# Where a VectorE block transposition stands in a group's order: slots 4 and 6, or slots 6 and 7

## The chip, the core and the metric

The kernel runs on one core of a Trainium2 chip. The metric is the device time of one execution in microseconds; lower is better. Before the change it is 1522.22 us, the median of three runs from 1521.25 to 1522.27.

The core has engines that work side by side, each with a queue of its own in program order: TensorE (PE, matrix products; PEld in the profile is its weight load), VectorE (DVE), ScalarE (ACT), GpSimd (POOL), and the queue of SyncE (SP), from which transfers are issued. They synchronise through semaphores. Products land in PSUM, which has eight banks.

## The reference

A batch is a matrix x of 128 nodes by 512 features; there are 128 batches. Two layers follow each other, both over the same adjacency matrix `adj` (128 x 128):

```python
h = jnp.maximum(_layernorm(x, axis=-1), 0.0)
x = x + _L0_gnn_ref(h, adj, adj, b0)      # W1 = W2 = adj
h = jnp.maximum(_layernorm(x, axis=-1), 0.0)
x = x + _L1_gnn_ref(h, adj, Wq, bq, Wk, bk, Wv, bv)
```

The first layer comes down to one number per node, `max(max_j (adj @ h)[i, j] + b0[i], 0)`, since A and C - A cancel but for the bias. Added to a whole row of x, it does not change that row's layer norm, so the second layer can use the same h. The second layer is attention with 8 heads of 64 over the 128 nodes, with scores masked where `adj` is zero: q, k and v are h times 512 x 512 weights.

## The kernel before

**Tiling.** Four batches are a group; there are 32 groups. The loop over g (lines 701 to 762) does, for each group: `apply` (weights times v of the group before, L600), `scores` (k times q, L570), and then the products that make v of group g and q and k of group g+1.

**Products.** A 512 x 512 projection of a group is cut into 2 x 2 quarters and done with seven quarter products instead of eight (class `Products`, lines 392 to 536; matmuls at L421, 128 x 256 each). Two of the seven, p4 and p3, are cut again into small blocks of 128 x 128 (`p43a` and `p43b`, matmuls at L487). The results are collected in PSUM banks and in the sum tile `u` by VectorE additions: L460 after p6, L469 after p7, L442 after p5 and at the end, and L490 (`more`), which adds a small block from the scratch bank 6 (`scr`) to `u`. Since `scr` is used several times, a small product into it must wait until the L490 addition of the one before has read it.

**Slots.** The work of a group is an explicit list `part` of 18 slots: v in slots 0 to 5, q in 6 to 11, k in 12 to 17. In each six stand p1, p6, p2, p7 with p43a, p5, p43b. In the first and the last group v has plain p7, p5, p4 and p3 instead of the block form. After the products of slot s, everything in `todo[s]` is issued. This is the order by hand in which each engine's queue gets its instructions: a matmul waits only for its data, but behind a VectorE instruction in the queue stands whatever was issued later.

**Side work in the slots.** While group g is computed, group g+2 is prepared. m = 4g + 8 is its first batch. `next_norms(m)` says in which slot each step of that stands, and is used as long as there is a group g+2, so in the first 30 groups:

- `norm` (L279 to L286): statistics on VectorE, then two small steps on GpSimd. `norm_end` (L289): the normalised rows with a relu on ScalarE, into tile `hn`.
- `add_bv` (L295, GpSimd): adds v's bias to x in place, for the sum at the end.
- `blocks` (L302, VectorE): transposes `hn` of one batch in blocks of 32 x 32 into tile `tb`.
- `move` (L312, SP): 16 transfers that bring the blocks of a pair of batches to their places in tile `hT`, so that `hT` holds the transposed matrix. It follows the second batch of a pair.
- `adjacency` (L327 on TensorE into bank 7, then the reduction L328 on VectorE).

In the same slots stand the masks of the attention weights (L582, on GpSimd, in the last groups on VectorE), the quarter sums of the next group (L345 on VectorE, L359 on GpSimd), loads of x (L229) and `add_c` (L626, ScalarE).

Of the kernel before, what the change touches and what calls it, by code (L numbers as in the profile page):

```python
# [167 lines left out]
def tile_adj_preln_d2(  # L168
# [38 lines left out]
    def fast(ctx):  # L207
# [436 lines left out]
        def next_norms(m):  # L644

            return {
                0: [(norm_end, m, False), (norm_end, m + 1, False)],
                4: [(blocks, m)],
                6: [(blocks, m + 1), (move, m + 1), (add_bv, m), (add_bv, m + 1)], 7: [(adjacency, m)],
                8: [(norm, m + 2), (norm_end, m + 2)],  # L650
                12: [(norm, m + 3), (norm_end, m + 3), (adjacency, m + 1)],
                13: [(blocks, m + 2)],
                14: [(blocks, m + 3), (move, m + 3), (adjacency, m + 2)],
            }

        with tc.manual_schedule():
# [44 lines left out]
            for g in range(NG):  # L701
# [16 lines left out]
                m = b + 2 * G  # L718
                if g + 1 < NG:
# [12 lines left out]
                    if g + 2 < NG:  # L732
                        for s, l in next_norms(m).items():
                            for what in l:
                                add(s, *what)
                    else:
                        add(6, count, 0, b)
# [73 lines left out]
```

## Time and profile before

| what | value |
|---|---|
| time, median of three runs | 1522.22 us |
| span of the profiled execution | 1519.2 us |
| one group in the middle (750.66 to 797.41) | 46.75 us |
| of it busy: TensorE, VectorE, ScalarE, GpSimd | 46.75, 31.62, 15.73, 26.66 us |
| transposition L302: count, median | 124, 701 ns |
| issues of `move` L312: count, median | 992, 609 ns |
| idle time of VectorE before L490, ended by L487 | 111.3 us in all |

"Busy" is the time in which an engine has an instruction running. The chain of waits follows the execution back from its end, at each step to what released it; its pieces in order of time show how long TensorE spent on each stretch of equal matmuls. The timeline lists single instructions: start in us from the span's start, length in us, engine, line, operation, output and inputs, and in brackets the idle time ahead of it and what ended it. A 32-bit matmul appears as two records, so that a quarter product of four matmuls reads "x8".

### The profile page before, as it was taken

How to read it: one execution, taken by the hardware profiler on the slowest of the kernel's cores; microseconds unless marked ns; L12 is line 12 of the kernel's file. 1: busy time of each engine (PE TensorE's matmuls, PEld its weight loads, DVE VectorE, ACT ScalarE, POOL GpSimd, SP SyncE). 2: the span in 40 equal slices, each digit the busy share in tenths (PEclk: the TensorE clock that was granted, in tenths of full speed). 3: DMA queues.
4: the chain of work that ended last, by engine and by line, in shares of the span. 5: the costliest groups of instructions: out<-in, count | busy, mean ns of one | idle time of the engine just before them, and what ended most of it. 6: DMA issues, size and time to landing. Idle time of an engine off the chain costs nothing.

```text
span 1519.2 us, 33036 instructions
## 1 busy us (share of the span) xinstructions
PE 1504.1 (99%) x12909; PEld 1325.6 (87%) x12909; DVE 1023.2 (67%) x2187; ACT 507.3 (33%) x970; POOL 844.4 (56%) x968
## 2 busy tenths in 40 slices
PE   8999999999999999999999999999999999999997
PEld 6888888888889888888888888888988888888886
DVE  6666666666666767666666666666676766666666
ACT  4333323333243332333332333324333233333232
POOL 5675656556565555654565655656555565456520
PEclk9999999999999999999999999999999999999999
DMA  5223222223222232222322222322223222222201
GB/s 170 58 65 80 59 65 74 65 76 75 52 73 67 73 83 43 76 66 74 80 58 65 75 65 76 73 54 73 66 73 84 43 76 76 64 80 57 52 32 58
DMA packets 307807, 105.32 MB, mean 69 GB/s; under 512 B 273153, under 2 KB 273281, under 8 KB 307649
## 3 DMA queue, kind: packets, MB, share of 16 engines
q1 hardware_dynamic: 307328, 102.84, 26.3%
q8 instruction: 104, 1.70, 0.5%
q14 instruction: 55, 0.44, 0.1%
q0 software_dynamic: 176, 0.27, 0.1%
q10 hardware_dynamic: 144, 0.07, 0.0%
HBM read 37.03 MB, written 33.55 MB: 46 GB/s over the span
## 4 chain that ended last, share of the span: by engine, by line
PE 99%; DVE 0%; DMA 0%; POOL 0%; ACT 0%; DVEq 0%; issue 0%
PE bk L421 55%; PE bk L487 19%; PE bk L600 8%; PE bk L570 8%; PE bk L327 7%; PE bk L546 1%; PE bk L321 0%; DMA xp<-in_x_dram 0%; DVE o L618 0%; ACT o L289 0%; DVE live L639 0%; DVE st L279 0%; DVE RS L617 0%; DVE o L630 0%; DVEq L776 0%; POOL rstd L284 0%
## 5 line engine op out<-in xcount | busy, mean ns | idle before, releaser
L630 POOL TENSOR_TENSOR o<-xp,o 128x512 f32<-128x512 f32 x122 | 151.1, 1268 | 312.7 <-DVE o L618 269.4
L582 POOL TENSOR_TENSOR w<-w,live 128x512 f32<-128x512 f32 x240 | 297.6, 1272 | 0.0
L490 DVE TENSOR_TENSOR u<-u,bk 128x256 f32<-128x256 f32 x552 | 205.7, 414 | 115.4 <-PE bk L487 111.3
L578 ACT ACTIVATE w<-bk 128x512 f32<-128x512 f32 x256 | 128.8, 625 | 345.6 <-PE bk L570 345.6
L295 POOL TENSOR_TENSOR xp<-xp,bv_sb 128x512 f32<-128x512 f32 x128 | 161.1, 1269 | 59.5 <-ACT hn L289 58.6
L421 PEld LDWEIGHTS bk<-hs,sk_sb 128*128 128x128 f32 x768 | 143.6, 190 | 44.7 <-issue 29.4
L421 PE MATMUL bk<-hs,sk_sb 128*128 128x256 f32 x768 | 181.3, 379 | 0.0
L421 PE MATMUL bk<-sv_sb,hs 128*128 128x256 f32 x768 | 181.2, 379 | 0.0
L421 PE MATMUL bk<-hs,sq_sb 128*128 128x256 f32 x744 | 175.8, 379 | 0.0
L421 PEld LDWEIGHTS bk<-sv_sb,hs 128*128 128x128 f32 x768 | 143.6, 190 | 31.1 <-issue 14.3
L328 DVE TENSOR_REDUCE amax<-bk 128x1 f32<-128x512 f32 x128 | 88.2, 689 | 105.4 <-PE bk L327 102.5
L359 POOL TENSOR_TENSOR h<-hT 128x256 f32<-128x256 f32 x31 | 22.6, 728 | 238.2 <-PE bk L487 233.8
L421 PEld LDWEIGHTS bk<-hs,sq_sb 128*128 128x128 f32 x744 | 138.9, 190 | 17.7
L469 DVE TENSOR_TENSOR u<-bk,u 128x512 f32<-128x512 f32 x95 | 65.8, 692 | 116.7 <-PE bk L421 114.6
L289 ACT ACTIVATE hn<-xp,nmr,rstd 128x512 f32<-128x512 f32 x124 | 100.8, 813 | 104.8 <-POOL nmr L286 104.8
L327 PE MATMUL bk<-hn,adjT 128*128 128x512 f32 x248 | 126.6, 592 | 0.0
L600 PE MATMUL bk<-v,w 128*64 128x65 f32 x4096 | 126.5, 222 | 0.0
L600 PEld LDWEIGHTS bk<-v,w 128*64 128x64 f32 x4096 | 122.1, 137 | 4.1 <-issue 0.3
L421 PE MATMUL bk<-wv_sb,hT 128*128 128x256 f32 x512 | 124.3, 386 | 0.0
L570 PE MATMUL bk<-qT,kT 64*128 64x128 f32 x2048 | 122.9, 275 | 0.0
L421 PE MATMUL bk<-hT,wk_sb 128*128 128x256 f32 x512 | 121.2, 380 | 0.0
L570 PEld LDWEIGHTS bk<-qT,kT 64*128 64x128 f32 x2048 | 116.8, 188 | 2.5 <-issue 0.3
(149 smaller groups left out, 2575.1 us busy)
## 6 DMA issues: line engine op xcount, KB each, us to landing
out_dram<-o SPq DMA_DIRECT2D x128, 256.0 KB, 2.0
xp<-in_x_dram SPq DMA_DIRECT2D x62, 512.0 KB, 3.9
hT<-tb SPq DMA_DIRECT2D x992, 32.0 KB, 1.9
xp<-in_x_dram SPq DMA_DIRECT2D x4, 256.0 KB, 4.4
wq_sb<-in_L_gnn_Wq_dram SPq DMA_DIRECT2D x2, 512.0 KB, 8.2
wk_sb<-in_L_gnn_Wk_dram SPq DMA_DIRECT2D x2, 512.0 KB, 9.8
wv_sb<-in_L_gnn_Wv_dram SPq DMA_DIRECT2D x2, 512.0 KB, 10.5
bv_sb<-in_L_gnn_bv_dram POOLq DMA_DIRECT2D x1, 256.0 KB, 6.7
```

The lines of the kernel that those rows point to most:

```text
L289: nc.scalar.activation(HN[m], x_of(m), AF.Relu, scale=RSTD[m], bias=NMR[m])
L295: nc.gpsimd.tensor_tensor(x_m, x_m, bv_sb, op=ALU.add)
L327: nc.tensor.matmul(pa, adjT, HN[m], start=True, stop=True)
L328: nc.vector.reduce_max(AMAX[g][:, i : i + 1], pa, axis=AX.X)
L421: nc.tensor.matmul(bank[:, r, :], lhs, rhs, start=first and r == 0 and c == 0, stop=r == 1 and c == 1, skip_group_check=True,)
L487: nc.tensor.matmul(out, lhs, rhs, start=start, stop=True, skip_group_check=True)
L490: nc.vector.tensor_tensor(to, to, what, op=ALU.add)
L570: nc.tensor.matmul(psc[j][:, f, :], KT[g][r, f, i * D : (i + 1) * D], QT[g][r, f, i * D : (i + 1) * D], start=True, stop=True,)
L578: nc.scalar.activation(w[:, j], psc[j], AF.Exp, scale=HD ** -0.5)
L582: eng.tensor_tensor(w[:, j], w[:, j], live_h, op=ALU.mult)
L600: nc.tensor.matmul(pav[r, c : c + HE], w[:, h % 2, h // 2, r], V[:, i, h, :], start=True, stop=True,)
L630: eng.tensor_tensor(y, x_of(b), y, op=ALU.add)
```

## The change

The transposition of batch m leaves slot 4 for slot 6, that of batch m+1 leaves slot 6 for slot 7. The `move` of the pair, which needs both, goes with the second. The two `add_bv` stay in slot 6. In VectorE's order this brings batch m's transposition from ahead of v's last L490 and L442 additions to behind them, and batch m+1's from ahead of q's p6 addition to behind it, ahead of the reduction of `adjacency(m)`. It is meant to keep VectorE free for the additions at the end of v, for which TensorE's products may have to wait. The transpositions of the other two batches (slots 13 and 14) stay.

```diff
             return {
                 0: [(norm_end, m, False), (norm_end, m + 1, False)],
-                4: [(blocks, m)],
-                6: [(blocks, m + 1), (move, m + 1), (add_bv, m), (add_bv, m + 1)], 7: [(adjacency, m)],
+                6: [(blocks, m), (add_bv, m), (add_bv, m + 1)],
+                7: [(blocks, m + 1), (move, m + 1), (adjacency, m)],
                 8: [(norm, m + 2), (norm_end, m + 2)],
                 12: [(norm, m + 3), (norm_end, m + 3), (adjacency, m + 1)],
                 13: [(blocks, m + 2)],
```

## The prediction

> **What bounds the kernel now.** I read the page's busy times and its chain first, then the chain in order of time over one group, then the timelines of TensorE and VectorE in that group.
>
> ```profile
> PE 1504.1 (99%) x12909; PEld 1325.6 (87%) x12909; DVE 1023.2 (67%) x2187; ACT 507.3 (33%) x970; POOL 844.4 (56%) x968
> PE 99%; DVE 0%; DMA 0%; POOL 0%; ACT 0%; DVEq 0%; issue 0%
> ```
>
> TensorE (PE) is busy 99% of the span and is 99% of the chain. The table of stretches says it more sharply: a group in the middle lasts 46.75 us, and PE is busy 46.75 us of it. VectorE (DVE) has 31.6 us, GpSimd (POOL) 26.7 and ScalarE (ACT) 15.7 of those 46.75. So nothing counts unless it shortens TensorE's own sequence. The list of waits names no steady wait of PE. But a matmul that is held up can hide in that busy time: the end of a record is modelled, and a piece of the chain runs to the next start. So I compared equal pieces. Here is one group in the chain in order of time (start, length, piece):
>
> ```profile
> 756.74 1.73 PE bk L421 x8
> 758.46 2.42 PE bk L487 x20
> 760.88 3.46 PE bk L421 x16
> ...
> 771.27 2.23 PE bk L487 x20
> ...
> 784.75 2.23 PE bk L487 x20
> ```
>
> The three pieces L487 x20 are the same work (`p43b`, ten 128x128 products, each recorded twice) for v, q and k. For v it takes 2.42 us, for q and k 2.23: 0.19 us too long. It repeats in every group from the second to the second-last; one q piece of the 30th group has 2.33. The timelines of DVE, PE and the weight loads (PEld), first at v's slots 4 and 5, then at q's slots 10 and 11:
>
> ```profile
> 758.50 0.69 DVE L442 TENSOR_TENSOR v<-bk,u 128x512 f32<-128x512 f32 x1 [0.65 <-PE bk L421]
> 759.11 0.70 DVE L302 STREAM_TRANSPOSE tb<-hn 128x512 f32<-128x512 f32 x1
> 759.74 0.38 DVE L490 TENSOR_TENSOR u<-u,bk 128x256 f32<-128x256 f32 x1
> 760.17 0.52 PEld L487 LDWEIGHTS bk<-ssv_sb,h 128*128 128x128 f32 x4
> 760.17 0.71 PE L487 MATMUL bk<-ssv_sb,h 128*128 128x128 f32 x4
> ...
> 771.31 0.69 DVE L442 TENSOR_TENSOR qT<-bk,u 128x512 f32<-128x512 f32 x1 [0.65 <-PE bk L421]
> 771.91 0.41 DVE L490 TENSOR_TENSOR u<-u,bk 128x256 f32<-128x256 f32 x1
> 772.78 0.53 PEld L487 LDWEIGHTS bk<-h,ssq_sb 128*128 128x128 f32 x4
> 772.89 0.61 PE L487 MATMUL bk<-h,ssq_sb 128*128 128x128 f32 x4
> ```
>
> In q the L490 addition follows p5's addition at once. It ends at 772.32, and the last products into bank 6 start undisturbed, the weight load 0.11 us before the matmul. In v the transposition of block m stands between. The addition, which reads bank 6, ends at 760.12. Only then, 0.05 us later, does the load of the next products into bank 6 start, together with its matmul. Undisturbed, the load would follow the one before (759.75) by 0.22 us, the spacing in this piece, at 759.97. So 0.20 us by these rounded times, 0.19 by the pieces: TensorE waits for VectorE here.
>
> **What the Trainium skill says.** "Perfetto Trace Analysis", section "Tensor Engine Instruction (MATMUL, LD_WEIGHTS)": the profiler estimates a matmul's end, and DVE, ACT and GpSimd queues are strict FIFO. The trace agrees: busy time equals the period although 0.19 us is lost, and the L490 addition doesn't start before the transposition ahead of it. "TensorE: Matmul & The Clock Gate", "Step-by-step: what each phase is for": PE may pull weight loads ahead of running matmuls, but matmuls keep program order. Here loads lead by 0.11 us, and at 760.17 the lead is zero. "SBUF — State Buffer", "Who interferes with whom": a DVE instruction with at most one SBUF input, outside the two-port modes, doesn't contend with GpSimd. The trace fits: GpSimd's 128x256 subtraction takes 0.73 us at 760.97 without a transposition beside it, and 0.73 us at 762.73 with one.
>
> **The change, part by part.**
>
> *Removed from slot 4.* In v's slots 4 and 5 DVE no longer has the transposition, 0.63 us from its start to that of the next instruction (759.11 to 759.74). The L490 addition starts at 759.11 and ends at about 759.5, against 759.92 that the weight load needs (759.97 less the 0.05 us of signalling): 0.4 us to spare, as in q. The hold of 0.19 us should go entirely. This counts for groups with the block form `p43b` in v and with `next_norms`. `next_norms` runs in the first 30 of 32 groups; the first has plain p4 and p3 in v, and its v pieces show no such hold. The 31st shows 2.42 too, but there a mask at slot 4 on DVE (0.68 us) holds the addition, and that mask stays. So 29 groups x 0.19 = 5.5 us.
>
> *Block m to slot 6.* It takes the very place of block m+1. The idle time there is 0.83 us, before the p6 addition at 764.44, and the transposition that stood ahead of it was there before too: zero. *The two `add_bv`* keep slot 6 and their place in GpSimd's order: zero.
>
> *Block m+1 to slot 7.* It now stands behind p6's addition and ahead of the reduction L328. Queued behind it:
>
> ```profile
> 764.44 0.69 DVE L460 TENSOR_TENSOR u<-bk,p1a 128x512 f32<-128x512 f32 x1 [0.83 <-PE bk L421]
> 765.23 0.69 DVE L328 TENSOR_REDUCE amax<-bk 128x1 f32<-128x512 f32 x1
> 765.84 0.68 DVE L279 BATCH_NORM_STATS2 st<-xp 128x6 f32<-128x512 f32 x1
> ...
> 768.76 0.69 DVE L469 TENSOR_TENSOR u<-bk,u 128x512 f32<-128x512 f32 x1 [1.76 <-PE bk L421]
> ```
>
> The p6 addition that TensorE needs for q.p7 stays ahead. The reduction and norm m+2 move 0.63 us later, and p7's addition had 1.76 us of idle time before it: 1.13 us are left, so it starts no later. The late reduction holds bank 7 to about 766.5; the next product into bank 7 is adjacency m+1 at 775.07: zero. The late norm moves rstd, nmr and the relu (768.02 to 768.65) and GpSimd's masks by 0.63. ACT's next work for TensorE is at 775.27. The five masks end at 776.97 instead of 776.35, which takes the 0.41 us that GpSimd waited before the next rstd (776.76) and moves that by 0.2 us. The relu of m+3 then ends at 778.7 instead of 778.52; its transposition starts at about 779.15, adjacency m+3 only in the next group. The last mask ends at 783.8 instead of 783.6; the application needs them from 786.9 on. All zero.
>
> *The move to slot 7.* Its 16 issues on the SP queue start when block m+1 is done: at 765.8 instead of 763.67, and take 11.2 us, to 777.0. The load behind them goes from 774.93 to 777.0 and lands after 3.9 us, at 781; its first reader is a statistic after 792. The next 16 issues at 779.85 wait for their own transposition; the queue is free at 777.6. The moved data are read in the next group. Zero. No operation is added or dropped, and a group should last 46.75 - 0.19 = 46.56 us.
>
> Sum: 1522.2 - 5.5 = 1516.7 us, 0.36% less. Rounding of the two pieces leaves 0.18 to 0.20 per group, 5.2 to 5.8 us.
>
> **Rivals.**
>
> *Only half comes back (1519.5).* Another wait could end just behind the first, say a bank-2 or bank-1 product waiting for p5's addition. For it: v's products swap the stationary and the moving side, so q is no exact twin. Against: inside v's piece all other spacings are 0.22 us, as in q's. 29 x 0.095 = 2.75 us off.
>
> *No change (1522.2).* The 0.19 us belongs to v's form and not to the transposition. For it: no v piece in block form lacks a long DVE operation at slot 4, so the trace has no direct counterexample. Against: the load starts 0.05 us after the addition's end, and the 31st group has the same hold behind a mask.
>
> *Slower (about 1535).* The second transposition becomes a new wait at slots 7 to 9: if the slack of 1.13 us before p7's addition did not exist and the full 0.63 us reached TensorE in 30 groups, +18.9 - 5.5 = +13.4 us, 1535.6. For it: that addition frees the bank into which the later block products go, and the norm chain through four engines shifts. Against: each of its links has 0.4 us or more to spare as worked out above, except the second rstd, whose 0.2 us falls into later slack.
>
> **How the numbers follow.** Forecast 0.84, half 0.06, no change 0.06, slower 0.04. The likeliest gives 1516.7. The range takes the forecast's bounds of 5.2 to 5.8 us, the scatter of 1 us of the three runs of before, and part of the way to the half gain: 1515.4 to 1518.7. Faster by over 0.2% (below 1519.2) is the forecast and a little of the half gain: 0.85. Within 0.2%: the rest of the half and no change, 0.11. Slower: 0.04.
>
> **What would show it.** In the changed kernel's chain the v piece L487 x20 should read 2.23 in groups 2 to 30 and still 2.42 in the 31st, and the stretch of one group should fall to 46.56. The addition L490 in v should follow p5's addition without a gap. The idle time before q's p7 addition should fall from 1.76 to about 1.13, still ended by PE. A v piece that stays at 2.42 refutes the cause; a q piece L487 x20 above 2.23, or a longer L421 piece at slots 7 to 9, would mean that the delay came back there.

## The result and the profile after

The changed kernel takes 1515.92 us (median of four runs, 1515.57 to 1516.45) against 1521.88 us before (median of four, 1521.25 to 1522.27). The ratio is 0.9962, 95% interval 0.9944 to 0.9979. The spans of the two profiles are 1519.2 and 1513.7 us, 5.5 us apart.

The chain in order of time, one group of the kernel after (start, length, piece):

```profile
800.65 1.73 PE bk L421 x8
802.38 2.23 PE bk L487 x20
804.61 3.46 PE bk L421 x16
...
814.99 2.23 PE bk L487 x20
...
828.47 2.23 PE bk L487 x20
```

The v piece, the first of the three L487 x20, now has the 2.23 us of the q and k pieces. Every other piece of the group has the length it had. In the table of stretches, a group lasts 46.56 us instead of 46.75. The same place in the timelines of VectorE, the weight loads and TensorE:

```profile
802.41 0.69 DVE L442 TENSOR_TENSOR v<-bk,u 128x512 f32<-128x512 f32 x1 [0.64 <-PE bk L421]
803.02 0.41 DVE L490 TENSOR_TENSOR u<-u,bk 128x256 f32<-128x256 f32 x1
803.89 0.53 PEld L487 LDWEIGHTS bk<-ssv_sb,h 128*128 128x128 f32 x4
804.00 0.61 PE L487 MATMUL bk<-ssv_sb,h 128*128 128x128 f32 x4
```

The L490 addition follows p5's addition at once and ends at 803.43. The next load into bank 6 starts at 803.89, with time to spare, and again leads its matmul by 0.11 us. Slot 7 in VectorE's timeline:

```profile
808.17 0.69 DVE L460 TENSOR_TENSOR u<-bk,p1a 128x512 f32<-128x512 f32 x1 [0.83 <-PE bk L421]
808.78 0.70 DVE L302 STREAM_TRANSPOSE tb<-hn 128x512 f32<-128x512 f32 x1
809.40 0.65 DVE L328 TENSOR_REDUCE amax<-bk 128x1 f32<-128x512 f32 x1
809.98 0.67 DVE L279 BATCH_NORM_STATS2 st<-xp 128x6 f32<-128x512 f32 x1
...
812.48 0.69 DVE L469 TENSOR_TENSOR u<-bk,u 128x512 f32<-128x512 f32 x1 [1.36 <-PE bk L421]
```

The moved transposition fills time in which VectorE was idle. q's p7 addition still waits 1.36 us for TensorE.

For the comparisons below the span is cut in three: the head up to group 2 (the start of its piece of 24 records L421), the middle from there to the start of the last run of products (56 records L421), and the end. The middle is the same work in all kernels and repeats to 0.02 us where it is unchanged. The head varied from 95.75 to 97.35 us between profiles, which is more than several of the differences in question.

| kernel | time, us | middle, us | v piece (L487 x20), us |
|---|---|---|---|
| before | 1521.88 | 1397.66 | 2.42 |
| after | 1515.92 | 1392.24 | 2.23 |

The middle lost 5.42 us: 0.187 us in each of 29 groups.

### The profile page after: what moved, and what is told of

Same layout as the page of the kernel before. It is cut to its first block, busy times and chain, and to the rows that moved or that the text cites. A ratio compares the mean times of both kernels' runs of the same rounds, so it can differ in the third digit from the quotient of the medians.

```text
span 1513.7 us, 33037 instructions
## 1 busy us (share of the span) xinstructions
PE 1498.6 (99%) x12909; PEld 1323.9 (87%) x12909; DVE 1020.5 (67%) x2187; ACT 506.9 (33%) x970; POOL 844.2 (56%) x968
## 4 chain that ended last, share of the span: by engine, by line
PE 99%; DVE 0%; DMA 0%; POOL 0%; ACT 0%; DVEq 0%; issue 0%
PE bk L421 55%; PE bk L487 19%; PE bk L600 8%; PE bk L570 8%; PE bk L327 7%; PE bk L546 1%; PE bk L321 0%; DMA xp<-in_x_dram 0%; DVE o L618 0%; ACT o L289 0%; DVE live L639 0%; DVE st L279 0%; DVE RS L617 0%; DVE o L630 0%; DVEq L776 0%; POOL rstd L284 0%
## 5 line engine op out<-in xcount | busy, mean ns | idle before, releaser
L490 DVE TENSOR_TENSOR u<-u,bk 128x256 f32<-128x256 f32 x552 | 206.7, 416 | 127.3 <-PE bk L487 123.1
L421 PEld LDWEIGHTS bk<-hs,sk_sb 128*128 128x128 f32 x768 | 143.6, 190 | 44.6 <-issue 29.2
L421 PE MATMUL bk<-hs,sk_sb 128*128 128x256 f32 x768 | 181.4, 379 | 0.0
L421 PE MATMUL bk<-sv_sb,hs 128*128 128x256 f32 x768 | 181.2, 379 | 0.0
L421 PE MATMUL bk<-hs,sq_sb 128*128 128x256 f32 x744 | 175.9, 379 | 0.0
L421 PEld LDWEIGHTS bk<-sv_sb,hs 128*128 128x128 f32 x768 | 143.7, 190 | 31.0 <-issue 14.3
L421 PEld LDWEIGHTS bk<-hs,sq_sb 128*128 128x128 f32 x744 | 139.0, 190 | 17.6
L421 PE MATMUL bk<-wv_sb,hT 128*128 128x256 f32 x512 | 124.3, 386 | 0.0
L421 PE MATMUL bk<-hT,wk_sb 128*128 128x256 f32 x512 | 121.1, 380 | 0.0
```

What stands on the lines that cost most here:

```text
L421: nc.tensor.matmul(bank[:, r, :], lhs, rhs, start=first and r == 0 and c == 0, stop=r == 1 and c == 1, skip_group_check=True,)
L490: nc.vector.tensor_tensor(to, to, what, op=ALU.add)
```

## The experiments

They ran in three sets, each with runs of the kernel before beside it on the same chip (medians 1521.19, 1521.43 and 1521.46 us).

**Block m alone to slot 6.**

```diff
-                4: [(blocks, m)],
-                6: [(blocks, m + 1), (move, m + 1), ...
+                6: [(blocks, m), (blocks, m + 1), (move, m + 1), ...
```

> Half of the change alone: block m goes from slot 4 to slot 6, block m+1 and the move stay in slot 6. My theory (the hold comes only from what stands ahead of v's L490 addition): the v piece L487 x20 falls to 2.23 in groups 2 to 30 and the whole gain is there, 1516.4 us against 1521.9. The two transpositions in slot 6 take 1.25 us; the 0.83 us of idle time before q's p6 addition was left with one of them, so 0.2 us remain and that addition starts no later. Rival (the second half of the edit, block m+1 behind p6's addition, brings or protects part of the gain): a q.p6 addition that starts late and a piece longer than 3.46 for the two products after it, 0.1 to 0.4 us a group, 1519 to 1528 us.

Measured: 1515.92 us, ratio 0.9965 (0.9952 to 0.9979), middle 1392.24, v piece 2.23. The whole gain is there. The limit of this half is seen in VectorE's timeline of this kernel:

```profile
760.62 1.29 DVE L302 STREAM_TRANSPOSE tb<-hn 128x512 f32<-128x512 f32 x2
762.16 0.69 DVE L460 TENSOR_TENSOR u<-bk,p1a 128x512 f32<-128x512 f32 x1 [0.24 <-PE bk L421]
```

With both transpositions ahead of it, p6's addition still waits for TensorE, but for 0.24 us instead of 0.83. Moving block m+1 to slot 7 as well widens this reserve and brings no time.

**Block m+1 and the move alone to slot 7.**

```diff
                 4: [(blocks, m)],
-                6: [(blocks, m + 1), (move, m + 1), (add_bv, m), (add_bv, m + 1)], 7: [(adjacency, m)],
+                6: [(add_bv, m), (add_bv, m + 1)],
+                7: [(blocks, m + 1), (move, m + 1), (adjacency, m)],
```

> The other half alone: block m stays in slot 4, block m+1 and the move go from slot 6 to slot 7. My theory: no change, 1521.9 us, v piece still 2.42, period 46.75. Rival (p6's addition or the transfers gain from the later place): a period below 46.75, 1516 to 1520 us.

Measured: 1521.4 us, ratio 1.0001 (0.9993 to 1.0009), middle 1397.67, v piece 2.42. This half does nothing, for better or worse.

**Another bank for the products that waited.**

```diff
+                if self.n == "v":
+                    scr = bank(7).rearrange("p (m k d) -> p m k d", m=2, k=2)
                 for k in range(2):
-                    self.block_mm(scr[:, 0, k], s[:, k, 1], t[:, k, 1])
+                    self.block_mm(scr[:, 0, k], s[:, k, 1], t[:, k, 1], start=self.n == "v" and k == 0)
```

> The order of before, with the transposition in slot 4; only the buffer is another: the last two small products of v's p43b go to bank 7 instead of the scratch bank 6, so that they need not wait for the L490 addition behind the transposition. My theory (TensorE waits for that addition to read bank 6): the v piece falls to 2.23, in the 31st group too, 1521.9 - 30 x 0.19 = 1516.2 us, with the late L490 addition unchanged in its place. Rival (the 0.19 us belongs to the form of v's products): 2.42 stays, 1521.9 us.

In bank 6 these products add to the partial sums that already stand there. In bank 7 the sums are missing, so v leaves out that part; the amount of work is the same. Measured: 1514.08 us, ratio 0.9953 (0.994 to 0.9967), middle 1392.05, v piece 2.23 in all groups, the 31st too. VectorE and the weight loads in this kernel:

```profile
756.31 0.70 DVE L302 STREAM_TRANSPOSE tb<-hn 128x512 f32<-128x512 f32 x1
756.93 0.38 DVE L490 TENSOR_TENSOR u<-u,bk 128x256 f32<-128x256 f32 x1
757.17 0.53 PEld L487 LDWEIGHTS bk<-ssv_sb,h 128*128 128x128 f32 x4
```

The transposition still stands in slot 4 and still delays the addition, which ends at 757.31. The load no longer waits for that end: it starts at 757.17, in the middle of the addition. So the transposition cost TensorE its 0.19 us through the reading of bank 6, and v's form costs nothing. The middle is 30 x 0.187 = 5.61 us shorter, as this theory says. From the 1521.19 us of its own set, 1515.6 was due; the time is 1.5 us less. That rest lies outside the middle and is taken up in the last run.

**Both transpositions in slot 4.**

```diff
-                4: [(blocks, m)],
+                4: [(blocks, m), (blocks, m + 1)],
-                6: [(blocks, m + 1), (move, m + 1), (add_bv, m), (add_bv, m + 1)], 7: [(adjacency, m)],
+                6: [(move, m + 1), (add_bv, m), (add_bv, m + 1)], 7: [(adjacency, m)],
```

> The suspected cause doubled: blocks m and m+1 both in slot 4, the move in slot 6. My theory: beyond 0.41 us of slack every us of VectorE work ahead of the L490 addition is a us of TensorE, so the hold is 2 x 0.63 - 0.41 = 0.85 instead of 0.19, v piece about 3.05, 29 x 0.63 = 18.3 us more than before: 1540 us. Rival (the hold is a fixed cost of any interruption there): 2.42 and 1521.9 us. Rival (part of the delay is absorbed by other work): 1525 to 1535 us.

Measured: 1538.84 us, ratio 1.0114 (1.0099 to 1.013), middle 1414.9: 17.24 us more than before, 0.59 in each of 29 groups, 0.78 us of hold in all. The first rival falls, and so does absorption: the second transposition goes to TensorE almost one for one. The transpositions and the addition in VectorE's timeline:

```profile
768.39 1.29 DVE L302 STREAM_TRANSPOSE tb<-hn 128x512 f32<-128x512 f32 x2
769.61 0.38 DVE L490 TENSOR_TENSOR u<-u,bk 128x256 f32<-128x256 f32 x1
```

A line of TensorE's waits in this kernel (us in total, times, longest):

```profile
PE bk L487 <- DVE u L490: 14.9, 29, 0.5
```

Its weight loads at this place:

```profile
769.03 0.30 PEld L487 LDWEIGHTS bk<-sv_sb,h 128*128 128x128 f32 x2
770.04 0.52 PEld L487 LDWEIGHTS bk<-ssv_sb,h 128*128 128x128 f32 x4 [0.71 <-DVE u L490]
```

With a hold this long, the wait gets a name and a releaser, the L490 addition. Even so the list shows 0.5 of the 0.78 us, since the modelled end of the matmul before covers the rest; the 0.19 us of the kernel before was covered completely.

**Half and three quarters of block m in slot 4.** In the changed kernel, `blocks` takes a range of the 128-column parts (2 or 3 of 4):

```diff
+                4: [(blocks, m, 0, 2)],        # three quarters: 0, 3
-                6: [(blocks, m), (add_bv, m), (add_bv, m + 1)],
+                6: [(blocks, m, 2, NC), (add_bv, m), (add_bv, m + 1)],
```

> The changed kernel, with half of block m (256 of 512 columns) transposed in slot 4 and the other half in slot 6. My theory (a slack of 0.41 us, estimated as 759.92 - 759.51, then one for one): half a transposition delays the next instruction by about 0.37 us, as the 128x256 additions L490 do, which is just inside the slack: v piece 2.23, 1516 us plus nothing. Rival (any VectorE instruction ahead of the addition costs its share): hold 0.1 us, v piece 2.32, 1518.8 us.

> The changed kernel, with three quarters of block m (384 of 512 columns) transposed in slot 4 and the last quarter in slot 6. My theory: the delay lies between 0.37 (half) and 0.63 (whole), about 0.50 us, of which 0.41 is slack: hold 0.09 us, v piece 2.32, 29 x 0.09 = 2.6 us above the changed kernel, 1518.5 us. Rival (a step at the whole transposition): 2.23 and 1515.9, or 2.42 and 1521.4 us.

Measured: 1516.57 us for half (ratio 0.9969, 0.9956 to 0.9981) and 1518.11 us for three quarters (0.9977, 0.9968 to 0.9986). The v pieces of groups 2 to 30 are 2.23 for half and 2.28 to 2.29 for three quarters, the middles 1392.34 and 1393.91. The 0.10 us by which half exceeds the changed kernel is a second q piece of 2.33. The two kernels have one line more, so L302 keeps its number and the addition is L491. The transposition in slot 4 and the addition behind it in VectorE's timeline, for half:

```profile
756.19 0.43 DVE L302 STREAM_TRANSPOSE tb<-hn 128x256 f32<-128x256 f32 x1
756.54 0.38 DVE L491 TENSOR_TENSOR u<-u,bk 128x256 f32<-128x256 f32 x1
```

And for three quarters:

```profile
758.53 0.57 DVE L302 STREAM_TRANSPOSE tb<-hn 128x384 f32<-128x384 f32 x1
759.03 0.38 DVE L491 TENSOR_TENSOR u<-u,bk 128x256 f32<-128x256 f32 x1
```

From start to start the delay is 0.35 and 0.50 us. With the whole and the double transposition there are four points:

| in slot 4 | delay of the addition, us | hold of TensorE, us | delay less hold, us |
|---|---|---|---|
| half | 0.35 | 0.00 | |
| three quarters | 0.50 | 0.06 | 0.44 |
| whole (before) | 0.63 | 0.19 | 0.44 |
| both | 1.22 | 0.78 | 0.44 |

A slack of 0.44 us and then one for one; the half, without a hold, is in keeping with it. I had estimated 0.41, with the 0.41 us that the L490 addition takes right behind p5's. Behind a transposition it takes 0.38, which is the difference. For three quarters I had expected 0.09 us, and 0.06 came.

**Both transpositions in slot 7.** In the changed kernel:

```diff
-                6: [(blocks, m), (add_bv, m), (add_bv, m + 1)],
-                7: [(blocks, m + 1), (move, m + 1), (adjacency, m)],
+                6: [(add_bv, m), (add_bv, m + 1)],
+                7: [(blocks, m), (blocks, m + 1), (move, m + 1), (adjacency, m)],
```

> The changed kernel with block m in slot 7 as well, ahead of block m+1: both transpositions between q's p6 addition and the reduction. My theory: the idle time before q's p7 addition was 1.36 us with one transposition there and falls to about 0.74, still positive, the chain of norm m+2 and the masks moves another 0.6 us and still ends in time: 1515.9 us, all pieces as in the changed kernel. Rival (the place in slot 7 is near a limit of its own): p7's addition is released by VectorE itself, or the transpositions of slots 13 and 14 wait for ScalarE, and TensorE pieces of q or k grow by 0.1 us or more, 1519 us or above.

Measured: 1516.85 us, ratio 0.9969 (0.9956 to 0.9982), middle 1392.24, to the hundredth that of the changed kernel. The idle time before q's p7 addition is 0.76 us, still ended by TensorE; the head of this profile was 1.1 us longer than that of after. Two transpositions fit in slot 7, so one was far from its limit.

**Bank 7 in the changed kernel.** The edit is that of the third run, with the same part left out.

> The changed kernel with the bank of the third run too: v's last two small products in bank 7. My theory: the hold is already gone in 29 groups and cannot be saved twice; only the 31st group's v piece, where a mask stands in slot 4, goes from 2.42 to 2.23: 1515.7 us, no difference that a timing can tell, and all v pieces 2.23. Rival (bank 7 saves something besides this hold): below 1515 us.

Measured: 1514.19 us, ratio 0.9949 (0.9933 to 0.9966), middle 1392.04. The hold can't be saved twice: the middle gains 0.20 us, the 31st group alone. But the time is again below 1515, where I had put the rival "something besides this hold". So the rival was right on the time; the middle shows that what is saved lies elsewhere, and the last run shows where.

**The mask of the 31st group.** The changed kernel, with one step more of the same kind:

```diff
-                    at = (8, 9, 9, 10, 10, 13, 14, 15) if m < B else (4, 8, 8, 12, 12, 13, 14, 14)
+                    at = (8, 9, 9, 10, 10, 13, 14, 15) if m < B else (8, 8, 8, 12, 12, 13, 14, 14)
```

> The changed kernel with one more step of the same kind: in the 31st group the mask that VectorE does in slot 4 goes to slot 8. My theory: that mask is the delay ahead of the addition there, so the 31st group's v piece falls from 2.42 to 2.23 and the end comes 0.19 us sooner, 1515.7 us, less than a timing can tell; the stretch from the second group to the last products shrinks from 1392.24 to 1392.05 us. Rival (in that group something else holds the piece): 2.42 stays.

Measured: 1516.09 us, ratio 0.9965 (0.9951 to 0.9978), middle 1392.05. The 31st group's v piece in the chain of the kernel after:

```profile
1454.37 2.42 PE bk L487 x20
```

And in this one:

```profile
1455.46 2.23 PE bk L487 x20
```

The mask did there what the transposition did elsewhere. The 0.19 us are real in the middle and lost in the scatter of the time.

**A longer TensorE program.** In the changed kernel, at the very start:

```diff
+        pd = bank(7)
+        for k in range(29):
+            nc.tensor.matmul(pd[0:1, k : k + 1], mhalf, mhalf, start=True, stop=True)
         pt = bank(0)
```

> A question left by the two runs with bank 7: they were 1.6 to 1.8 us faster than the hold explains, and in their profiles this lies after the last VectorE instruction (4.0 and 5.0 us to the end instead of 5.4 to 5.9). Their TensorE program is 29 instructions longer. Here the changed kernel gets 29 products of 1x1 at its very start, where TensorE waits for the identity matrix, and nothing else. If the length of TensorE's program sets the end (its instructions are fetched by transfers that run beside the last output): a tail of 4 to 5 us and about 1514.2 us. If not: a tail of 5.4 to 5.9 us and 1515.9 us, or 0.3 more where the head gets longer, and the cause of those 1.7 us stays open.

Measured: 1514.34 us (1513.53 to 1515.79), ratio 0.9954 (0.9941 to 0.9968), middle 1392.24. That is 1.75 us below the median of the mask run on the same chip, which is the changed kernel but for 0.19 us; the slowest run here, 1515.79, is just below the fastest there, 1515.82. It has 29 products more and nothing less. From the last VectorE instruction to the end it takes 4.5 us, against 5.7 after. SP's last wait in the kernel after (us in total, times, longest):

```profile
SPq L806 <- DMA out_dram<-o: 2.6, 1, 2.6
```

In the third run:

```profile
SPq L808 <- DMA out_dram<-o: 0.9, 1, 0.9
```

And in this one:

```profile
SPq L809 <- DMA out_dram<-o: 1.4, 1, 1.4
```

The program's end waits for the last output transfer, and less long in the three kernels whose TensorE program is longer: by 29 products here (58 weight loads and 58 matmuls in the records), by 29 semaphore instructions in the two with bank 7. The packets in the traces show more. Besides the output's queue, q1, the page lists queues of the kind "instruction". One of them, q8, moves 104 packets of 16 KB in every kernel. In the kernel after, the packets that start from 1508.85 to 1510.85 us and from 1510.85 to 1512.85 us include these (queue, kind: packets, MB, share of the 16 DMA engines):

```profile
q8 instruction: 1, 0.02, 5.7%
q1 hardware_dynamic: 9, 0.02, 3.3%
```

The q8 packet runs from 1509.11 to 1510.93 us. All other packets of the output have ended by 1509.84. The last nine, eight of 2 KB and a closing one of 4 bytes, start only at 1510.89 and end at 1511.90. Eight of 2 KB are a sixteenth of a 256 KB transfer, so by an estimate the part of one of the 16 DMA engines. In this kernel, from 1504.00 to 1506.00 us and from 1510.57 to 1512.57 us:

```profile
q8 instruction: 1, 0.02, 2.9%
q1 hardware_dynamic: 2, 0.00, 0.1%
```

Here the q8 packet is over at 1505.28 us, before the last four output transfers are issued from 1506.02 on, and only two packets of 4 bytes start after 1510.57. The split is the same in all twelve traces. In the nine kernels without the longer TensorE program, the last eight 2 KB packets start 0.8 to 1.5 us after the 2 KB packet before them and within 0.04 us of a q8 packet's end; in the other three, no 2 KB packet of the last transfer follows more than 0.3 us after the one before. More instructions on other engines don't do it: the two split kernels have 30 more on VectorE, the one with both transpositions in slot 7 has 30 more on ScalarE, and their last waits are 2.3 to 2.7 us. So a part of the last output stands behind a packet of instructions, and the longer TensorE program brings that packet forward, out of the way. That q8 carries TensorE's program is inferred from this comparison; no trace names it. Other lengths were not run, so this is no rule that a longer program ends sooner.

This kernel keeps the whole computation, and its median is the lowest of those that do.

## Why the prediction was right

I said 1516.7 us in a range from 1515.4 to 1518.7, and 1515.92 came. Step by step:

- *TensorE alone sets the time, and the 0.19 us in v's piece is a hold by the addition behind the transposition.* Shown three ways: take the transposition away (block m alone), leave it and take the bank away, double it. v's form, the rival "no change", falls with the second. "Only half comes back" falls with the v piece, which is down to the 2.23 us of q and k.
- *0.19 us x 29 groups = 5.5 us.* The middle lost 5.42, 0.187 per group. The first group saved nothing, and the 31st kept 2.42 behind its mask until the mask moved.
- *The slack of 0.4 us.* 0.44, from three points; the half, with 0.35 us of delay and no hold, fits.
- *Block m in slot 6 costs nothing.* The idle time before p6's addition is 0.83 us, as before.
- *Block m+1 in slot 7 costs nothing.* Right, but a term was mis-sized: I took the whole 0.63 us from the idle time of q's p7 addition and expected 1.13 us; 1.36 was left. What follows shifted by about 0.4 us. Before, the reduction had itself started 0.79 us after p6's addition, since it waited for TensorE's adjacency product. Behind the transposition that product is long done, and the next two instructions follow at 0.62 and 0.58 us.
- *The second rstd moves by 0.2 us.* Wrong, from the same mis-sized term: it did not move. Delayed by 0.4 us and not 0.63, the five masks used up just the 0.41 us for which GpSimd had waited there. The rstd starts 12.32 us after q's p6 addition in both kernels (776.76 and 764.44 before, 820.49 and 808.17 after). The transpositions of slots 13 and 14 stand where they stood, and k's piece is 2.23.
- *The move to slot 7 costs nothing.* Right. Its 16 issues took 10.4 us instead of the 11.2 that I had carried over, so the load of x behind them follows 0.7 us earlier than I had reckoned.
- *The q piece of 2.33 in the 30th group* stayed. The two split kernels have two such pieces instead, in the 2nd and the 18th group, and none in the 30th; why is open. Each is 0.1 us in the whole run.
- *Half the gain, slower:* no piece of the middle grew.

The medians fell by 5.96 us, half a microsecond more than the middle. The profiles of the two kernels have heads of 96.16 and 96.13 us and ends of 25.38 and 25.33 us, so nothing in them accounts for it. I take it for scatter: runs of one kernel differ by 1 us here and by up to 2.5 us in the experiments. The start of my sum, 1522.2 us, was itself on the high side of it: the kernel before has medians of 1521.19 to 1521.46 us in the three sets, from which 1515.92 is 5.3 to 5.5 us less.

## What to carry to other kernels

When an engine is busy 100% of the time, compare equal pieces of its chain: a piece that is longer in one place than its twins in another hides a wait that no list names. Then look at what stands ahead of the releaser in its queue, and move that to a place where the queue is idle, after counting the reserve there. Compare a small gain over the part of the span that repeats, since head and end vary by more; here a change of TensorE's program length alone moved the end by more than 1 us.

## What was not expected of the hardware

- A hold of TensorE by 0.19 us left no entry among the waits, and one of 0.78 us was listed with 0.5.
- 29 products of 1x1 at the start made the run 1.75 us shorter (1516.09 to 1514.34 us, medians of five runs each). The last eight 2 KB packets of the output no longer start 0.8 to 1.5 us late, behind a 16 KB packet of instructions, as they do in the nine kernels without a longer TensorE program.
- A transposition of 32-bit data costs VectorE's queue 0.35, 0.50 and 0.63 us for 256, 384 and 512 columns: about 0.07 us for each further 64 columns, and, as an estimate from these three, some 0.07 us of fixed cost.
